# Cross-attention on one core: most of the context turned by VectorE from block loads, Wv turned into a tile of its own, one G product moved ahead of a group of transposes

## The chip, the core and the metric

The kernel runs on one core of a Trainium2 chip. The metric is the device time of one execution in microseconds (us), the median of several runs. One of the executions was also recorded by the hardware profiler; the span of its trace (first to last instruction) is somewhat shorter than the execution's time.

## What is computed

The layer is a cross-attention with eight heads, a residual and a layer norm, all in fp32. There are B = 16 batches, S = 256 queries of DI = 256 features, S2 = 77 context rows of DL = 192 features per batch, and a head size D = 256.

```python
Q = (x @ Wq).reshape(B, -1, H, D).transpose(0, 2, 1, 3)
K = (ctx @ Wk).reshape(B, -1, H, D).transpose(0, 2, 1, 3)
V = (ctx @ Wv).reshape(B, -1, H, D).transpose(0, 2, 1, 3)
score = where(mask, einsum('bhqd,bhkd->bhqk', Q, K) / sqrt(D), -inf)
attn = softmax(score)
out = einsum('bhqk,bhkd->bqhd', attn, V).reshape(B, -1, H * D) @ Wo + x
return layer_norm(out) * gamma + beta
```

The mask is all ones in the inputs, but the kernel reads and applies it.

## The kernel before

The kernel never forms Q, K or V. For each head it forms G = Wk_h Wq_h^T / 16 (192 x 256) and U = Wv_h Wo_h (192 x 256) once. Then a = G^T c^T gives the scores x a, and vw = c U gives what the softmax weights multiply. The 192 context features are split into a part of 128 rows (tiles `gA`, `uA`, `cA`) and a part of 64 rows. In the part of 64 rows two heads share the 128 partitions (`gB`, `uB`), and `cB` holds the 64 context rows twice, in its upper and its lower partitions. So both G and U need their weights turned, and the products need the context turned: features on partitions, (batch, context row) along the free dimension, 16 x 77 = 1232 columns.

Each engine runs its instructions in the order in which the program writes them (a manual schedule), and all loads are issued by SyncE (SP) in program order. At most eight of its transfers are outstanding, since the transfer eight places later waits for the semaphore of the one before. The program has a set-up part and a loop.

The set-up, up to the call of `prepare_last` (L822), goes in this order on TensorE (PE):

- `keep_busy`, then transposes on PE of Wk and Wq of heads 0, 1, 4 and 5: `turn_k`, `turn_q`, `turn_k_last` (one bank of four 128 x 128 transposes each, into PSUM, copied out by `evacuate` at L148, which alternates between ScalarE and VectorE). The G product of heads 0 and 1 (`g_of(0)`) stands after `turn_k(1)`, the transposes of Wk of heads 4 and 5.
- `turn_c(0, first)` (L651): the first three blocks of 112 context rows (`c_sb`, loaded at L568), which hold the first four batches, are turned by six PE transposes, copied to `cA` and the lower half of `cB`, and GpSimd (POOL) copies the lower half to the upper (L668). Then `g_of(1)` and `rest_of_g`.
- the other heads' Wk and Wq were loaded in 32-row blocks (`load_blocks` L563) and are turned by VectorE in 32 x 32 blocks (`turn_blk` L644) into tiles of their own, `kT_blk` and `qT_blk`. `a_of_places((0, 1))` forms a of four heads for batches 0 to 3 (tile `pa`), `of_pair` (L676) and `rest_of_pairs` (L688) form the other G (tiles `pgb`, `phb`), `turn_v` (L670) turns Wv in place, and `a_of_places((2, 3))` follows.
- `turn_c(first, NCR)` (L783): the other eight blocks of context rows are turned by 16 PE transposes (tile `pc`) with eight evacuations and four POOL copies. Then POOL copies the last 13 context rows of every batch to `cRA` and `cRB` (L784, L785), clears `vr` (L786) and makes the mask bias (L790).
- `of_pair` and `rest_of_pairs` again, for U (tiles `pu` and `pw`), with `wvT` as weights. They are copied to `uA` and `uB`; POOL copies each half of `uB` to the other partitions (L809), forms two sums in each of `uA` and `uB` (L812, L813), and finishes the bias (L816 to L818), which also needs a maximum by VectorE (L815).
- VectorE turns the first queries (`transpose_x` L172), and `prepare_last` (L267) multiplies `uA` with `cRA` and `uB` with `cRB` for the last 13 context rows of all batches (tile `pr`: part A of one half of the heads, part B of both, part A of the other) and copies the result to `vr`.

In-place turning of Wv reads and writes every fourth column:

```python
        def turn_v(a):
            blocks = wvT[:, a].rearrange("p m (c n) -> p m n c", n=4)
            nc.vector.transpose(blocks, blocks)
```

and the weights of `pu` and `pw` are then read with a step of four elements (16 bytes):

```python
            return flat(wvT[half(e), a]).rearrange("p (l n) -> p n l", n=4)[:, n]
```

The loop (from L833) takes one batch per turn: `scores` (tile `ps`) of two tiles of 128 queries, the bias and maximum (`shift`), softmax, vw of the batch, a of the next group of four batches, the weighted sum, and the layer norm. The program text of the loop does not differ between the two kernels.

The order of the loads on SP is: Wk and Wq of heads 0, 1, 4, 5 (L571 to L575), the first context blocks (L568), 16 block loads of Wk and Wq (L565), the other context blocks (L568), 16 block loads of Wv (L565), four of Wo (L594), the mask for all 128 partitions (L595), four of the first queries `xT` in 32-row blocks (L168), then `xg` (L144), gamma, beta and the next group's queries.

Of the kernel before, what the change touches and what calls it, by code (L numbers as in the profile page):

```python
# [8 lines left out]
F32 = mybir.dt.float32  # L9
I32 = mybir.dt.int32  # L10
AF = mybir.ActivationFunctionType
ALU = mybir.AluOpType
# [3 lines left out]
P = 128  # L16
H = 8
D = 256
EPS = 1e-05
GB = 4  # L20
KM = 64
MASKED = 3.0e38
# [31 lines left out]
def kernel(  # L54
# [13 lines left out]
    nc = tc.nc  # L68
    B, S, DI = x.shape
    S2, DL = c.shape[1], c.shape[2]  # L70
    LB = DL - P
    CR = 112
    NCR = B * S2 // CR
    NG = B // GB
    QT = S // P
    NT = B * QT
# [5 lines left out]
    NL = DL // BK  # L82
    PW = (NF + 1) * BK
    assert KM == 2 * BK and NM == NF and 2 * KR <= BK
    assert NCR * CR == B * S2 and NG * GB == B and DI == 2 * P and D == 2 * P and 2 * LB == P


    engines = mybir.EngineType
# [33 lines left out]
    vr = const.tile([P, B, DI], F32, tag="vr", name="vr")  # L122
# [144 lines left out]
    def prepare_last():  # L267


        pr = [ps_mm.tile([P, 2, B, KR], F32, tag="mm", name=f"pr_{n}") for n in range(DI // BK)]  # L270

        def part_A(e):
            for n, o in enumerate(pr):
                nc.tensor.matmul(  # L274
                    o[:, e].rearrange("p b k -> p (b k)"),
                    flat(of_e(uA, e)[:, n]),
                    flat(cRA),
                    start=(e == 0),
                    stop=(e == 1),
                )  # L280

        def part_B(e):
            for n, o in enumerate(pr):
                nc.tensor.matmul(  # L284
                    o[:, e].rearrange("p b k -> p (b k)"),
                    flat(of_e(uB, e)[half(n % 2), n]),
                    flat(cRB[half(n % 2)]),
                    start=(e == 1),
                    stop=(e == 0),
                )  # L290
# [253 lines left out]
    early = ctx.enter_context(tc.tile_pool(name="early", bufs=1))  # L544
    pools[0] = turned = early
    with tc.tile_pool(name="wonce", bufs=1) as wp:
        c_sb = wp.tile([CR, NCR, DL], F32, tag="c", name="c_sb")


        wq_nat = wp.tile([P, 2, 2, 2 * D], F32, tag="w128", name="wq_nat")  # L550
# [16 lines left out]
        def load_c(lo, hi):  # L567
            nc.sync.dma_start(c_sb[:, lo:hi, :], c_rows[:, lo:hi, :])  # L568

        first = -(-GB * S2 // CR)  # L570
        nc.sync.dma_start(wk_nat[:, 0], wk_rows[0][:, : 2 * D])  # L571
        nc.sync.dma_start(wq_nat[:, 0], wq_rows[0][:, :, : 2 * D])
        nc.sync.dma_start(wk_nat[:, 1], wk_rows[1][:, : 2 * D])
        nc.sync.dma_start(wq_nat[:, 1], wq_rows[1][:, :, : 2 * D])
        nc.sync.dma_start(wk_last, wk_ends[:, : 2 * D])  # L575
        load_c(0, first)
        for e in range(2):
            load_blocks(wk_blk[:, e], wk_blocks[2 * e + 1])
            load_blocks(wq_blk[:, e], wq_blocks[2 * e + 1])
        load_c(first, NCR)  # L580

        warm = const.tile([P, 1], F32, tag="warm", name="warm")
        nc.scalar.activation(warm, eps, AF.Exp)
# [8 lines left out]
            load_blocks(wvT[:, a], wv_blocks[a])  # L592
        for a in range(NF):
            nc.sync.dma_start(wo_of[a // 2][:, a % 2], wo_rows[a])  # L594
        nc.sync.dma_start(  # L595
            bias_f.bitcast(I32), mask.rearrange("b k -> (b k)").partition_broadcast(P)
        )
# [24 lines left out]
        def turn_q(e, u):  # L622
            chunks = [
                wq_nat[:, e, t, u * D + dc * P : u * D + (dc + 1) * P]
                for dc in range(2) for t in range(2)
            ]
            pt = turn_chunks(chunks, f"q_{e}_{u}")
            evacuate(flat(qT[:, e, u]), flat(pt))

        def turn_k(e):  # L630
            pt = turn_chunks([wk_nat[:, e, n * P : (n + 1) * P] for n in range(4)], f"k_{e}")
            evacuate(
                kT[:, e].rearrange("p u n l -> p (u n) l")[:, :, :P], pt
            )
# [13 lines left out]
                    blk[:, e].rearrange("p m (n c) -> p m n c", c=BK),  # L648
                )

        def turn_c(lo, hi):  # L651
            for r in range(lo, hi, 2):
                n = min(2, hi - r)
                pc = ps_mm.tile([P, 4, P], F32, tag="mm", name=f"pc_{r}")
                for lc in range(2):
                    for j in range(n):
                        nc.tensor.transpose(  # L657
                            pc[:, 2 * lc + j, :CR],
                            c_sb[:, r + j, lc * LB : lc * LB + P],
                            ident[:CR, :CR],  # L660
                        )
                rows = slice(r * CR, (r + n) * CR)
                evacuate(flat(cA)[:, rows].rearrange("p (j m) -> p j m", m=CR), pc[:, :n, :CR])
                evacuate(
                    flat(cB)[LB:, rows].rearrange("p (j m) -> p j m", m=CR),
                    pc[LB:, 2 : 2 + n, :CR],
                )
                nc.gpsimd.tensor_copy(flat(cB)[:LB, rows], flat(cB)[LB:, rows])  # L668

        def turn_v(a):  # L670
            blocks = wvT[:, a].rearrange("p m (c n) -> p m n c", n=4)
            nc.vector.transpose(blocks, blocks)

        def of_pair(out, a, weight, moving):  # L676

            for n in range(4):
                for e in range(2):
                    nc.tensor.matmul(  # L680
                        out[e][:, a % 2, :],
                        weight(a, e, n)[:, :P],
                        moving(a, e, n),
                        start=(n == 0),
                        stop=(n == 3),
                    )
# [23 lines left out]
            return kT_blk[half(e), a, n]  # L710

        def wv_part(a, e, n):
            return flat(wvT[half(e), a]).rearrange("p (l n) -> p n l", n=4)[:, n]

        def wo_part(a, e, n):
            return wo_of[a // 2][half(e), a % 2, n, :]
# [1 line left out]
        def g_of(e):  # L718

            pg = ps_mm.tile([P, 2, DI], F32, tag="mm", name=f"pg_{e}")  # L720
            for u in range(2):
                for dc in range(2):
                    nc.tensor.matmul(
                        pg[:, u],
                        kT[:, e, u, dc, :P],
                        qT[:, e, u, dc],
                        start=(dc == 0),
                        stop=(dc == 1),
                    )
            nc.scalar.mul(gA[:, NF * e : NF * e + 2], pg, D ** -0.5)  # L730
# [23 lines left out]
        keep_busy(4)  # L754
        turn_q(0, 0)
        turn_q(0, 1)
        turn_k(1)
        g_of(0)
        turn_q(1, 0)
        turn_q(1, 1)  # L760
        turn_k_last()
        turn_c(0, first)
        g_of(1)
        rest_of_g(0)
        rest_of_g(1)
# [14 lines left out]
        nc.sync.dma_start(bet, beta.partition_broadcast(P))  # L780
        a_of_places((2, 3))
        turn_v(3)
        turn_c(first, NCR)  # L783
        nc.gpsimd.tensor_copy(cRA, cA[:, :, KM:])  # L784
        nc.gpsimd.tensor_copy(cRB, cB[:, :, KM:])  # L785
        nc.gpsimd.memset(vr, 0.0)  # L786

        nc.gpsimd.tensor_scalar(bias_f, bias_f.bitcast(I32), 0.0, -MASKED, ALU.is_equal, ALU.mult)  # L790

        for j in range(NF // 2):
            pu = two_banks("pu", j)
            for a in range(2 * j, 2 * j + 2):
                of_pair(pu, a, wv_part, wo_part)
            for e in range(2):
                evacuate(
                    of_e(uA, e)[:, :, 2 * j : 2 * j + 2].rearrange("p n a c -> p a n c"),
                    pu[e].rearrange("p a (n c) -> p a n c", c=BK),
                )  # L800
        for j in range(NF // 2):
            for e, pw in enumerate(
                rest_of_pairs(j, (2 * j, 2 * j + 1), wv_part, wo_part, "pw")
            ):
                for i, engine in enumerate((nc.scalar.copy, nc.vector.tensor_copy)):
                    a = 2 * j + i
                    here, there = (of_e(uB, e)[half(k), :, a] for k in (i, 1 - i))
                    engine(here, pw[half(i)].rearrange("p (n c) -> p n c", c=BK))
                    nc.gpsimd.tensor_copy(there, here)  # L809
# [12 lines left out]
        prepare_last()  # L822


# [131 lines left out]
```

## Time and profile before

| what | value |
|---|---|
| median of three runs | 280.88 us (280.25 to 281.27) |
| the profiled execution's own time | 279.81 us |
| span of its trace | 278.0 us |
| granted TensorE clock, mean | 0.993 |
| PE busy | 269.4 us (97%) |
| VectorE (DVE) busy | 206.6 us (74%) |
| ScalarE (ACT) busy | 166.6 us (60%) |
| GpSimd (POOL) busy | 167.8 us (60%) |
| moved by DMA | 22.61 MB |

The profiled execution takes 1.81 us more than its span and 1.07 us less than the median. "L680" is line 680 of the kernel before. PEld is the loading of a matmul's weights, which can run beside the matmul before it; a matmul in fp32 appears as two records. A wait is put down to the semaphore that came last. A DMA's time to landing runs from its issue to its semaphore.

### The profile page before, as it was taken

The numbers are of one execution on the slowest core, as the hardware profiler recorded it, in microseconds if no ns is written. First come the engines' busy times: TensorE is split into PE (matmuls) and PEld (weight loads), VectorE is DVE, ScalarE is ACT, GpSimd is POOL, SyncE is SP. The second block draws the span as 40 slices with busy tenths as digits, with TensorE's granted clock in tenths as the row PEclk, the third lists the DMA queues.
The fourth block names the chain that finished last, engine by engine and source line by source line (L and its number), as shares of the span: only waits on it lengthen the run. The fifth ranks groups of instructions, "written<-read, shape, count | busy, mean of one in ns | idle before, by whom it ended". The sixth has DMA issues, their size and how long they took to land.

```text
span 278.0 us, 13274 instructions
## 1 busy us (share of the span) xinstructions
PE 269.4 (97%) x5924; PEld 194.2 (70%) x5924; DVE 206.6 (74%) x423; ACT 166.6 (60%) x447; POOL 167.8 (60%) x226
## 2 busy tenths in 40 slices
PE   7999999999999999999999999999999999999991
PEld 6756499976595959585868686868677767575650
DVE  0463952777838898878889787778788887788785
ACT  2303232146638676767767676868585857869761
POOL 1000069946677777787877878777777536335274
PEclk9999999999999999999999999999999999999997
DMA  6997999930000100950100109500001010010103
GB/s 192 249 230 154 308 261 238 204 105 4 2 6 2 35 10 24 189 174 4 42 2 5 41 5 193 180 16 22 24 2 42 2 40 14 31 41 2 40 4 113
DMA packets 35641, 22.61 MB, mean 81 GB/s; under 512 B 17712, under 2 KB 34048, under 8 KB 35584
## 3 DMA queue, kind: packets, MB, share of 16 engines
q1 hardware_dynamic: 35440, 21.64, 30.8%
q8 instruction: 46, 0.75, 1.2%
q10 hardware_dynamic: 144, 0.13, 0.1%
q14 instruction: 11, 0.09, 0.1%
HBM read 17.57 MB, written 4.19 MB: 78 GB/s over the span
## 4 chain that ended last, share of the span: by engine, by line
PE 89%; DVE 4%; DMA 3%; ACT 2%; SPq 1%; POOL 0%; issue 0%; POOLq 0%; ACTq 0%
PE ps L313 23%; PE pa L199 12%; PE pv L241 9%; PE po L429 9%; PE pm L429 7%; PE pa L213 6%; PE pv L252 6%; PE po L378 5%; DMA c_sb<-in_ctx_dram 3%; PE pu L680 3%; PE pr L274 2%; ACT e L342 2%; PE pw L694 1%; PE pgb L680 1%; PE pr L284 1%; PE pc L657 1%
## 5 line engine op out<-in xcount | busy, mean ns | idle before, releaser
L342 ACT ACTIVATE e<-s,top 128x77 f32<-128x77 f32 x256 | 67.1, 347 | 52.1 <-DVE top L335 49.9
L356 POOL TENSOR_TENSOR p<-e,rden 128x512 f32<-128x512 f32 x64 | 45.9, 739 | 46.5 <-DVE rden L350 46.3
L313 PE MATMUL ps<-a,xT 128*32 128x154 f32 x2048 | 70.0, 294 | 0.0
L313 PEld LDWEIGHTS ps<-a,xT 128*32 128x32 f32 x2048 | 66.1, 110 | 1.7 <-issue 0.7
L328 DVE TENSOR_TENSOR s<-ps,bias 128x308 f32<-128x308 f32 x64 | 30.3, 475 | 17.6 <-PE ps L313 15.9
L199 PE MATMUL pa<-cA,gA 128*32 128x308 f32 x512 | 35.8, 423 | 0.0
L462 POOL TENSOR_TENSOR xg<-xg,m 128x256 f32<-128x256 f32 x33 | 24.2, 734 | 13.5 <-DVE xg L476 11.8
L199 PEld LDWEIGHTS pa<-cA,gA 128*32 128x32 f32 x512 | 16.4, 110 | 20.9 <-issue 8.0
L241 PE MATMUL pv<-uA,cA 128*32 128x512 f32 x256 | 30.4, 592 | 0.0
L366 DVE STREAM_TRANSPOSE pT<-p 128x640 f32<-128x640 f32 x32 | 25.6, 824 | 2.4 <-POOL p L356 2.4
L348 DVE TENSOR_REDUCE den<-e 128x8 f32<-128x616 f32 x32 | 24.7, 772 | 3.5 <-ACT e L342 3.5
L335 DVE TENSOR_REDUCE top<-s 128x8 f32<-128x616 f32 x32 | 25.4, 795 | 1.1
L668 POOL COPY cB<-cB 64x224 f32<-64x224 f32 (+1 forms) x6 | 1.9, 360 | 35.2 <-DVE cB L153 35.2
L392 POOL TENSOR_TENSOR ts<-vw 128x768 f32<-128x768 f32 x11 | 22.0, 1997 | 0.0
L213 PE MATMUL pa<-cB,gB 64*32 64x308 f32 x512 | 19.5, 420 | 0.0
L378 PE MATMUL po<-vw,pT 128*32 128x256 f32 x320 | 19.2, 380 | 0.0
L863 ACT COPY vw<-pv 128x512 f32<-128x512 f32 x32 | 16.9, 579 | 2.5 <-PE pv L252 2.5
L495 ACT ACT_TABLE_LOAD x14 | 18.0, 1283 | 0.3
L213 PEld LDWEIGHTS pa<-cB,gB 64*32 64x32 f32 x512 | 9.7, 107 | 11.3 <-issue 7.6
L252 PE MATMUL pv<-uB,cB 64*32 64x512 f32 x256 | 17.4, 601 | 0.0
L516 DVE SCALAR_TENSOR_TENSOR xg<-xg,mv,gam 128x256 f32<-128x256 f32 x25 | 17.2, 688 | 0.0
L378 PEld LDWEIGHTS po<-vw,pT 128*32 128x32 f32 x320 | 10.0, 110 | 9.5 <-DVE den L348 2.5
(115 smaller groups left out, 444.0 us busy)
## 6 DMA issues: line engine op xcount, KB each, us to landing
xT<-in_x_dram SPq DMA_DIRECT2D x16, 256.0 KB, 6.1
xg<-in_x_dram SPq DMA_DIRECT2D x4, 1024.0 KB, 7.6
out_dram<-xg SPq DMA_DIRECT2D x15, 256.0 KB, 2.3
wo<-in_L_xattn_Wo_dram SPq DMA_DIRECT2D x4, 512.0 KB, 5.9
wvT<-in_L_xattn_Wv_dram SPq DMA_DIRECT2D x16, 96.0 KB, 3.0
wq_nat<-in_L_xattn_Wq_dram SPq DMA_DIRECT2D x2, 512.0 KB, 6.0
wq_blk<-in_L_xattn_Wq_dram SPq DMA_DIRECT2D x8, 128.0 KB, 4.7
wk_blk<-in_L_xattn_Wk_dram SPq DMA_DIRECT2D x8, 96.0 KB, 5.5
```

The lines of the kernel that those rows point to most:

```text
L199: nc.tensor.matmul(flat(o[i * BK : (i + 1) * BK]), gA[:, h, cols(dc, i)], flat(cA[:, batches, :]), start=not B_first, stop=B_first,)
L213: nc.tensor.matmul(flat(banks[j + k][i * BK : (i + 1) * BK]), gB[half(k), h % NF, cols(dc, i)], flat(cB[half(k), batches, :]), start=B_fir ...
L241: nc.tensor.matmul(pv[k][i * BK : (i + 1) * BK], cA[:, b, k * BK : (k + 1) * BK], uA[:, parts, :, i], start=True, stop=False,)
L252: nc.tensor.matmul(pv[k][i * BK : (i + 1) * BK], cB[half(k), b, k * BK : (k + 1) * BK], uB[half(k), parts, :, i], start=False, stop=True,)
L313: nc.tensor.matmul(ps[m // 2][i * BK : (i + 1) * BK, m % 2 * 2 * S2 : (m % 2 + 1) * 2 * S2], xT_of[g][:, j * NM + m, dc], flat(a_of[g][:, ...
L328: nc.vector.tensor_tensor(s[:, a * H // 2 : (a + 1) * H // 2], ps[a][:, : H // 2 * S2].rearrange("p (h k) -> p h k", k=S2), bias[:, b, :]. ...
L335: nc.vector.tensor_reduce(top, s, AX.X, ALU.max, negate=True)
L342: nc.scalar.activation(e[:, h], s[:, h], AF.Exp, bias=top[:, h : h + 1])
L356: nc.gpsimd.tensor_tensor(part, e_mh[:, :, :, keys], rden_mh.unsqueeze(3).to_broadcast(list(part.shape)), ALU.mult,)
L366: nc.vector.transpose(pT_of[t].rearrange("p n m q -> p m n q"), p.rearrange("p m (n k) -> p m n k", k=BK),)
L378: nc.tensor.matmul(po[i * BK : (i + 1) * BK], pT[:, n, i], vw_of[b][:, 2 - n // 2 * 2 : 4 - n // 2 * 2, n % 2, :] if n < NF else vr[:, b, ...
L429: nc.tensor.matmul(out[i * BK : (i + 1) * BK], weight[:, i], moving, start=(n == 0), stop=(n == len(terms) - 1),)
```

## The change

There are three edits, and some moves that go with them.

1. The context's rest (the 896 rows after the first three blocks of 112) is no longer loaded as rows and turned on PE. Six loads of 32-row blocks, one for each 32 of the 192 features, bring it straight into the columns of `cA` (four loads) and the lower half of `cB` (two loads), in pieces of 32 elements (128 bytes). Two VectorE transposes of 896 columns turn these columns in place, POOL makes the upper half of `cB` by one copy of 64 x 896, and `cRA` and `cRB` follow. The loads stand after those of Wo; the turning stands between the U products of the second pair and their evacuation.
2. `turn_v` writes its result to a new tile `wv_turned`, in which the weights of each product lie side by side. That tile takes the memory of `vr`; `vr` comes into being after U is done, and only the columns that nothing else writes are cleared (6 of every 32), by VectorE instead of POOL.
3. `g_of(0)` stands ahead of `turn_k(1)`.

The bias's first step goes from POOL to VectorE, behind the evacuations of `pu`; POOL's last bias steps go ahead of its sums in `uA` and `uB`.

```diff
@@ loads
+        rest = slice(first * CR, None)
+        def load_rest():
+            blocks = c.rearrange("b k l -> (b k) l")[rest].rearrange("(m r) l -> r m l", r=BK)
+            for l in range(NL):
+                i, of = (l, cA) if l < NM else (l - NM + LB // BK, cB)
+                nc.sync.dma_start(
+                    flat(of)[i * BK : (i + 1) * BK, rest].rearrange("p (m q) -> p m q", q=BK),
+                    blocks[:, :, l * BK : (l + 1) * BK],
+                )
+
+        def turn_rest():
+            nc.vector.transpose(flat(cA)[:, rest], flat(cA)[:, rest])
+            nc.gpsimd.tensor_copy(cRA, cA[:, :, KM:])
+            nc.vector.transpose(flat(cB)[LB:, rest], flat(cB)[LB:, rest])
+            nc.gpsimd.tensor_copy(flat(cB)[:LB, rest], flat(cB)[LB:, rest])
+            nc.gpsimd.tensor_copy(cRB, cB[:, :, KM:])
...
-        load_c(0, first)
+        nc.sync.dma_start(c_sb, c_rows[:, :first, :])
         for e in range(2):
             load_blocks(wk_blk[:, e], wk_blocks[2 * e + 1])
             load_blocks(wq_blk[:, e], wq_blocks[2 * e + 1])
-        load_c(first, NCR)
...
             nc.sync.dma_start(wo_of[a // 2][:, a % 2], wo_rows[a])
+        load_rest()
         nc.sync.dma_start(
             bias_f.bitcast(I32), mask.rearrange("b k -> (b k)").partition_broadcast(P)
         )
@@ Wv
+        wv_turned = const.tile([P, NF, 4, DL], F32, tag="vr", name="wv_turned")
         def turn_v(a):
-            blocks = wvT[:, a].rearrange("p m (c n) -> p m n c", n=4)
-            nc.vector.transpose(blocks, blocks)
+            nc.vector.transpose(
+                wv_turned[:, a].rearrange("p n (m r) -> p m n r", r=BK),
+                wvT[:, a].rearrange("p m (c n) -> p m n c", n=4),
+            )
...
-            return flat(wvT[half(e), a]).rearrange("p (l n) -> p n l", n=4)[:, n]
+            return wv_turned[half(e), a, n]
@@ order
         turn_q(0, 1)
+        g_of(0)
         turn_k(1)
-        g_of(0)
...
         a_of_places((2, 3))
         turn_v(3)
-        turn_c(first, NCR)
-        nc.gpsimd.tensor_copy(cRA, cA[:, :, KM:])
-        nc.gpsimd.tensor_copy(cRB, cB[:, :, KM:])
-        nc.gpsimd.memset(vr, 0.0)
-        nc.gpsimd.tensor_scalar(bias_f, bias_f.bitcast(I32), 0.0, -MASKED, ALU.is_equal, ALU.mult)
         for j in range(NF // 2):
             pu = two_banks("pu", j)
             for a in range(2 * j, 2 * j + 2):
                 of_pair(pu, a, wv_part, wo_part)
+            if j:
+                turn_rest()
             for e in range(2):
                 evacuate(
                     of_e(uA, e)[:, :, 2 * j : 2 * j + 2].rearrange("p n a c -> p a n c"),
                     pu[e].rearrange("p a (n c) -> p a n c", c=BK),
                 )
+        nc.vector.tensor_scalar(bias_f, bias_f.bitcast(I32), 0.0, -MASKED, ALU.is_equal, ALU.mult)
...
-        for u in (uA, uB):
-            t2, _, b22, b11, b12 = (u[:, q].rearrange("p n i c -> p (n i c)") for q in range(5))
-            nc.gpsimd.tensor_tensor(t2, b22, b12, ALU.subtract)
-            nc.gpsimd.tensor_tensor(t2, t2, b11, ALU.add)
         nan = wp.tile([P, B, 1], F32, tag="nan", name="nan")
         nc.vector.tensor_reduce(nan[:, :, 0], bias, AX.X, ALU.max)
         nc.gpsimd.tensor_tensor(nan, nan, nan, ALU.mult)
         nc.gpsimd.tensor_tensor(nan, nan, nan, ALU.subtract)
         nc.gpsimd.tensor_tensor(bias, bias, nan.to_broadcast([P, B, S2]), ALU.add)
+        for u in (uA, uB):
+            t2, _, b22, b11, b12 = (u[:, q].rearrange("p n i c -> p (n i c)") for q in range(5))
+            nc.gpsimd.tensor_tensor(t2, b22, b12, ALU.subtract)
+            nc.gpsimd.tensor_tensor(t2, t2, b11, ALU.add)
         for j in range(0, GT, 2):
             transpose_x(0, j)
+        vr = const.tile([P, B, DI], F32, tag="vr", name="vr")
+        ends = flat(vr).rearrange("p (n c) -> p n c", c=BK)[:, :, 2 * KR :]
+        nc.vector.memset(ends, 0.0)
         prepare_last()
```

More of the change, by code (lines that the diff above doesn't have):

```diff
@@ L72 @@
     CR = 112
-    NCR = B * S2 // CR
     NG = B // GB
@@ L84 @@
     assert KM == 2 * BK and NM == NF and 2 * KR <= BK
-    assert NCR * CR == B * S2 and NG * GB == B and DI == 2 * P and D == 2 * P and 2 * LB == P
+    assert NG * GB == B and DI == 2 * P and D == 2 * P and 2 * LB == P
     engines = mybir.EngineType
@@ L121 @@
     cRB = const.tile([P, B, KR], F32, tag="cRB", name="cRB")
-    vr = const.tile([P, B, DI], F32, tag="vr", name="vr")
     p_ring = [const.tile([P, NM, PW], F32, tag=f"p{i}", name=f"p_{i}") for i in range(2)]
@@ L546 @@
     with tc.tile_pool(name="wonce", bufs=1) as wp:
-        c_sb = wp.tile([CR, NCR, DL], F32, tag="c", name="c_sb")
+        first = -(-GB * S2 // CR)
+        c_sb = wp.tile([CR, first, DL], F32, tag="c", name="c_sb")
         wq_nat = wp.tile([P, 2, 2, 2 * D], F32, tag="w128", name="wq_nat")
@@ L565, in load_blocks @@
                 nc.sync.dma_start(to[i * BK : (i + 1) * BK], blocks[i])
-        def load_c(lo, hi):
-            nc.sync.dma_start(c_sb[:, lo:hi, :], c_rows[:, lo:hi, :])
-        first = -(-GB * S2 // CR)
+        rest = slice(first * CR, None)
+        assert (B * S2 - first * CR) % BK == 0
+        def load_rest():
[12 more added lines that the diff above has]
+            nc.gpsimd.tensor_copy(cRB, cB[:, :, KM:])
         nc.sync.dma_start(wk_nat[:, 0], wk_rows[0][:, : 2 * D])
@@ L649, in turn_blk, with turn_c @@
                 )
-        def turn_c(lo, hi):
-            for r in range(lo, hi, 2):
-                n = min(2, hi - r)
+        def turn_c():
+            for r in range(0, first, 2):
+                n = min(2, first - r)
                 pc = ps_mm.tile([P, 4, P], F32, tag="mm", name=f"pc_{r}")
@@ L761 @@
         turn_k_last()
-        turn_c(0, first)
+        turn_c()
         g_of(1)
```

## The prediction

> **What bounds the kernel now.** I read the chain of work that ended last first, because a busy share says nothing of which wait ends last. PE has 89% of it. These are its pieces in order of time (start, length, what; all us):
>
> ```profile
> 3.12 8.36 DMA c_sb<-in_ctx_dram
> 11.48 0.04 issue
> 11.53 0.80 PE pc L657 x6
> ...
> 22.46 3.65 PE pgb L680 x32
> ...
> 34.52 1.68 PE pc L657 x16
> 36.20 7.77 PE pu L680 x64
> 43.98 3.68 PE pw L694 x64
> 47.65 3.01 PE pr L274 x16
> 50.66 3.01 PE pr L284 x32
> 53.68 3.01 PE pr L274 x16
> 56.69 4.33 PE ps L313 x128
> ```
>
> Up to 11.53 the chain is the load of the first context blocks. From there to 258 each PE piece begins where the one before it ends, so an instruction taken off PE in that stretch shortens the span by its own length, if what follows it is ready that much sooner. The piece at 34.52 is the 16 transposes that go.
>
> Then the groups by line, shapes kept apart, of the stretch 0 to 62 us (busy us, mean ns of one, idle before):
>
> ```profile
> L680 PE MATMUL pu<-wo,wvT 64*128 64x256 f32 x64 | 7.8, 400 | 0.0
> L680 PEld LDWEIGHTS pu<-wo,wvT 64*128 64x128 f32 x64 | 7.5, 325 | 0.1
> L672 DVE STREAM_TRANSPOSE wvT<-wvT 128x768 f32<-128x768 f32 x4 | 6.4, 1644 | 0.0
> L680 PE MATMUL pgb<-qT_blk,kT_blk 64*128 64x256 f32 x32 | 3.7, 382 | 0.0
> L680 PEld LDWEIGHTS pgb<-qT_blk,kT_blk 64*128 64x128 f32 x32 | 3.0, 187 | 0.8 <-ACT a L151 0.5
> L646 DVE STREAM_TRANSPOSE kT_blk<-wk_blk 128x768 f32<-128x768 f32 x2 | 1.9, 950 | 0.0
> ```
>
> `pu` and `pgb` are the same products but for the weights' step of four elements in `pu`: its weight loads take 325 ns and not 187, and in the chain one of its matmuls takes 7.77/64 = 121 ns and not 3.65/32 = 114. The transposes of L672 and L646 differ in the same way.
>
> Last, the timeline and the busy time by stage (length, PE, PEld, DVE, ACT, POOL, clock, DMA share, GB/s) for what must supply PE:
>
> ```profile
> 42.77 4.39 POOL L790 TENSOR_SCALAR bias<-bias 128x1232 f32<-128x1232 int32 x1
> 47.21 3.59 POOL L809 COPY uB<-uB 64x256 f32<-64x256 f32 x8
> ```
>
> ```profile
> 24.00:26.00 2.00, 2.00 (x20) 1.55 (x16) 0.00 (x0) 0.00 (x0) 0.00 (x0) 1.00 0.26 69
> 26.00:28.00 2.00, 2.00 (x38) 1.20 (x40) 0.00 (x0) 1.09 (x2) 0.00 (x0) 1.00 0.59 161
> 34.00:36.00 2.00, 2.00 (x33) 1.54 (x16) 1.96 (x4) 1.67 (x5) 0.00 (x0) 1.00 1.03 413
> 38.00:40.00 2.00, 2.00 (x20) 2.00 (x20) 0.03 (x1) 0.00 (x0) 1.94 (x5) 1.00 1.37 173
> ```
>
> POOL's eight `uB` copies begin only after its 4.39 us of bias and end at 50.8, just as part B of `pr` (50.66) needs them: a PE that is earlier finds them late unless POOL is relieved too. The DMA engines are nearly idle from 24 to 28, and a stretch of 256-byte pieces (38 to 40, `xT`) moves 173 GB/s where big pieces move 413.
>
> [...]loads 74% longer cost only 6% of spacing. [...]The trace has 512-byte pieces at 228 GB/s (mean of 14 to 22 us), which is 16 x 512/228 = 36 ns per piece and engine, and 256-byte pieces at 177 GB/s (38 to 44), 23 ns; none of 128 bytes.
>
> **The change, part by part.**
>
> *The 16 transposes go.* 1.68 us of PE on the path. Their eight evacuations and four POOL copies lay beside it. What is next: `pu` at 34.52 needs Wo, turned Wv and two free banks. Wo arrives at about 30.4 (below). The three Wv transposes that precede the `a` copies on DVE begin at 28.73 and end by 33.7 at today's price; the first `a` copies, 0.42 to 0.46 us, free both banks by 34.2. Nothing is late: -1.68.
>
> *Wv in a tile of its own.* `pu` at the spacing of `pgb`: 64 x 114 = 7.30 us, -0.47. `pw` today has 3.68/64 = 57 ns, and its like with contiguous weights (`phb`, 1.89/32 = 59) is no faster: 0. Bounds: 0 (if the spacing has another reason) and -0.6. I take -0.47. The DVE transposes still read with the step, write without it: 950 to 1644 ns, beside PE either way.
>
> *G of heads 0 and 1 earlier.* Today PE works from 7.26 to 11.02 and then waits 0.51 for the context blocks. Moved ahead, `pg` waits for the copy of `qT`, which ends at 7.44 on DVE and 7.78 on ACT. If all of it waits for the second, the same 3.76 us end at 11.54, as the load lands: 0, worst +0.1. Without the load as cover it could save 0.3.
>
> *The loads.* On SP the one context load ahead of Wv goes, six come behind Wo, ahead of mask, `xT`, `xg`, gamma and beta. The old one is 0.69 MB, 3.0 us at 228 GB/s; without it the eight-transfer limit no longer holds Wv back (SP waits 3.0 us for it today), so the idle 2.3 us (0.74 and 0.41 of two 2 us windows) fill too. Wo ends today at about 35.7 (413 GB/s holds until then), hence at 30.4. The new loads are 6 x 896 = 5376 pieces. Price per piece and engine: on the line through 36 and 23 ns it is 16; [...]no cheaper than 256 bytes, 23[...]. I take 23: 5376 x 23/16 = 7.7 us. `cA` (two thirds) is in at 35.5, `cB` at 38.1, the mask (1.6 us) at 39.7, `xT` (5.9 us) at 45.6. xg, gamma, beta and the second `xT` are used after 75 us: covered.
>
> *DVE, at the new times* (`pu` 34.5 to 41.8, `pw` to 45.5, `pr` B at 48.5, `ps` at 54.5). `uA` copy until 38.9; the turn of 896 columns costs 950 + 128 x 1.07 (slope to the 1225 ns of 1024 columns) = 1.09 us, twice: 40.0 and 41.1; `uA` 41.9 to 42.6; bias on DVE [...]1.44 us (the reduce of the same 1232 columns), I take 1.4: 44.0; four `uB` copies (0.42) are done 1.2 us after `pw` ends, 46.7; maximum 1.44, four `xT` turns 0.67 each: 50.9; clearing 768 columns 0.66 at POOL's 3.51 us for 4096, I take 0.8: 51.7. `vr` copies, first 0.6 us, must precede `ps`: slack 2.2. So cA is needed at 38.9, cB at 40.0, the mask at 42.6, xT at 48.2: slack 3.4, 1.9, 2.9 and 2.6. Queued behind a late load would be `uA`, bias and `uB` copies, for which `pr` waits.
>
> *POOL.* `vr` clearing (3.51) and bias (4.39) go. `cRA` 0.36 at 40.4; the `cB` copy of 896 columns 1.09 (283 ns for 112, 398 for 224) at 42.2; `cRB` 42.6; eight `uB` copies of 0.40 from 44.2: 47.4, needed 48.5, slack 1.1. Then two small steps and the bias (2.25) by 51.0, needed 56.7; the `uA` sums by 53.6, needed 58.9; the `uB` sums by 56.1, needed 62.7. All covered: 0.
>
> *Sum.* -1.68 - 0.47 = -2.15. The profiled execution of 279.81 (span 278.0) would be 277.66 (span 275.85). It lies 1.07 below the median; from the median, 280.88 - 2.15 = 278.7.
>
> **The rivals.** (a) Only the transposes pay; `pu` keeps 121 ns: 279.2. For it: weight loads overlap and matmuls of 393 ns hide much. Against: `pgb` with the same matmul has 114. (b) The cover is partly gone: pieces at 37 to 43 ns, or DVE later by 1 to 3 us than reckoned, eat a part: 278.7 to 280.9, middle 279.9. (c) Slower: the small pieces cost the doubled 46 ns. The six loads take 15.5 us, `cB` is in at 45.9, and on POOL its turn, copy, `cRB` and eight copies (1.09 + 1.09 + 0.36 + 3.2) follow: `pr` B begins at 51.6, not 48.5. `xT` comes at 53.4, its turns, clearing and first copy end at 57.5: the same delay. 3.1 lost against 2.15 gained: 281.8. Loss begins at 37 ns and outweighs the gain from 43 ns. [...]Against: 256-byte pieces[...] cost less than 512-byte ones. (d) A little more than the sum, by spacing or a start on an earlier load: 278.1.
>
> **How the numbers follow.** Forecast 0.67 (278.2 to 279.3, with the spread of runs), (a) 0.12, (b) 0.10, (c) 0.07, (d) 0.04. From 277.9 to 279.9 lie forecast, (a), (d) and half of (b), 0.88; closer ends would cut into the bounds of `pu` and the run spread. A measurement can tell 0.3% (0.84 us) from no change: faster than 280.04 are forecast, (a), (d) and half of (b), 0.88; half of (b) and a part of (c) within, 0.07; slower 0.05.
>
> **What would show it.** `pu` should begin near 34.5 straight after `pa` and take 7.3; weight loads near 187 ns; DVE should wait for no load ahead of its turns; `pr` B follow A with no gap; `ps` begin near 54.5. Wrong: a DVE wait on `cA`, `cB`, `bias` or `xT`, a gap ahead of `pr` or `ps`, or `pc` later than 11.6.

## The result, and the profile after

The changed kernel takes 278.28 us (median of six runs, 277.25 to 279.10), the kernel before in the same session 280.69 (280.25 to 281.27). The ratio is 0.9907 with a 95% interval of 0.9884 to 0.9931: 2.41 us less. The forecast from 280.88 was 278.7, range 277.9 to 279.9. The profiled execution took 277.25 us with a span of 275.5 (before: 279.81 and 278.0; reckoned: 277.66 and 275.85), at a mean granted clock of 0.995. Executions over 1.5% above the fastest of their kernel count as a slower state and are left out of the figures below: three of 22 with the bias on POOL, three of 20 with the spare loads, and one of the kernel before, at 992 us.

The chain of the work that ended last, after the change (start, length, what; us):

```profile
3.13 8.38 DMA c_sb<-in_ctx_dram
...
11.56 0.79 PE pc L673 x6
...
22.49 3.65 PE pgb L701 x32
...
34.55 7.11 PE pu L701 x64
41.66 3.61 PE pw L715 x64
45.28 3.01 PE pr L272 x16
48.29 3.01 PE pr L282 x32
51.30 3.01 PE pr L272 x16
54.31 4.32 PE ps L311 x128
```

The start and the stretch up to 34.5 are as before. The piece of 16 transposes is gone and nothing has taken its place: `pu` follows `pa` directly. `pu` has become 0.66 shorter and `pw` 0.07. The scores begin at 54.31 instead of 56.69, 2.38 earlier: -1.68 - 0.66 - 0.07, and +0.03 from the start. From there to its end this trace takes 221.2 us (275.5 - 54.31), the one before 221.3.

The groups of 0 to 62 us, shapes kept apart (busy us, mean ns of one, idle before):

```profile
L701 PE MATMUL pu<-wo,wv_turned 64*128 64x256 f32 x64 | 7.2, 379 | 0.0
L690 DVE STREAM_TRANSPOSE wv_turned<-wvT 128x768 f32<-128x768 f32 x4 | 6.2, 1600 | 0.0
L701 PEld LDWEIGHTS pu<-wo,wv_turned 64*128 64x128 f32 x64 | 6.1, 187 | 1.2 <-ACT a L149 0.5
```

A weight load of `pu` takes 187 ns instead of 325, the price of `pgb`. But the four VectorE turns of Wv still take 1600 ns each (1644 before), although they now write contiguously.

Last, the timeline of the new supply (start, length, what, idle before), and SP's issue of the loads:

```profile
38.89 1.10 DVE L581 STREAM_TRANSPOSE cA<-cA 128x896 f32<-128x896 f32 x1
40.02 1.11 DVE L583 STREAM_TRANSPOSE cB<-cB 64x896 f32<-64x896 f32 x1
42.46 0.80 DVE L818 TENSOR_SCALAR bias<-bias 128x1232 f32<-128x1232 int32 x1
44.09 3.58 POOL L827 COPY uB<-uB 64x256 f32<-64x256 f32 x8 [1.49 <-ACT uB L826]
48.22 3.08 PE L282 MATMUL pr<-cRB,uB 64*128 64x208 f32 x32
49.01 2.49 DVE L173 STREAM_TRANSPOSE xT<-xT 128x512 f32<-128x512 f32 x4 [1.05 <-DMA xT<-in_x_dram]
```

```profile
15.91 9.51 SPq L564 DMA_DIRECT2D wvT<-in_L_xattn_Wv_dram  x16
25.46 1.86 SPq L609 DMA_DIRECT2D wo<-in_L_xattn_Wo_dram  x4
27.37 7.23 SPq L575 DMA_DIRECT2D cA<-in_ctx_dram  x4
34.64 1.83 SPq L575 DMA_DIRECT2D cB<-in_ctx_dram  x2
36.52 0.54 SPq L611 DMA_DIRECT2D bias<-in_mask_BxS_if_dram  x1
```

DVE waits for none of `cA`, `cB` and the mask, but for `xT`, 1.05 us. Such a wait was one of the prediction's signs of being wrong; here it costs PE nothing. POOL ends the `uB` copies at 47.67, 0.55 before part B of `pr` needs them.

### The profile page after: what moved, and what is told of

Read it like the earlier page. It is cut to its first block, busy times and chain, and to the rows that moved or that the text cites. A ratio compares the mean times of both kernels' runs of the same rounds, so it can differ in the third digit from the quotient of the medians.

```text
span 275.5 us, 13238 instructions
## 1 busy us (share of the span) xinstructions
PE 267.7 (97%) x5908; PEld 192.2 (70%) x5908; DVE 208.9 (76%) x423; ACT 165.4 (60%) x443; POOL 159.5 (58%) x221
## 4 chain that ended last, share of the span: by engine, by line
PE 89%; DVE 4%; DMA 3%; ACT 2%; SPq 1%; POOL 1%; issue 0%; POOLq 0%; ACTq 0%
PE ps L311 24%; PE pa L197 12%; PE pv L239 9%; PE po L427 9%; PE pm L427 8%; PE pa L211 6%; PE pv L250 6%; PE po L376 5%; DMA c_sb<-in_ctx_dram 3%; PE pu L701 3%; PE pr L272 2%; ACT e L340 2%; PE pgb L701 1%; PE pw L715 1%; PE pr L282 1%; PE phb L715 1%
## 5 line engine op out<-in xcount | busy, mean ns | idle before, releaser
L326 DVE TENSOR_TENSOR s<-ps,bias 128x308 f32<-128x308 f32 x64 | 30.4, 475 | 17.6 <-PE ps L311 17.5
L197 PEld LDWEIGHTS pa<-cA,gA 128*32 128x32 f32 x512 | 17.2, 110 | 20.1 <-issue 7.7
L884 ACT COPY a<-pa 128x308 f32<-128x308 f32 x48 | 16.6, 447 | 0.0
```

What stands on the lines that cost most here:

```text
L197: nc.tensor.matmul(flat(o[i * BK : (i + 1) * BK]), gA[:, h, cols(dc, i)], flat(cA[:, batches, :]), start=not B_first, stop=B_first,)
L326: nc.vector.tensor_tensor(s[:, a * H // 2 : (a + 1) * H // 2], ps[a][:, : H // 2 * S2].rearrange("p (h k) -> p h k", k=S2), bias[:, b, :]. ...
L884: nc.scalar.copy(dst, src)
```

## The experiments

The theory: the gain is the 16 transposes (1.68) and the closer spacing of `pu`, on a path where PE never waits; it holds only while the small loads, DVE's queue and POOL's copies stay under cover. The rivals: the transposes alone pay; or the loads or POOL are the real limit. Medians of one kernel differ by some tenths of a us from the runs' spread, and the start differs more: `pc` begins at anything from 11.24 to 13.68 us, as the first loads land. So where a trace can tell, I compare the stretch from the first `pc` to the first `ps`; it is 54.31 - 11.56 = 42.75 us in the changed kernel and 56.69 - 11.53 = 45.16 us in the kernel before, 2.41 less. The medians, too, differ by 2.41 us (280.69 and 278.28). For a median of an experiment the kernel before of the same session is given beside it.

**Wv turned in place again** (weights with a step of four elements; all else as changed).

```diff
-            nc.vector.transpose(
-                wv_turned[:, a].rearrange("p n (m r) -> p m n r", r=BK),
-                wvT[:, a].rearrange("p m (c n) -> p m n c", n=4),
-            )
+            blocks = wvT[:, a].rearrange("p m (c n) -> p m n c", n=4)
+            nc.vector.transpose(blocks, blocks)
...
-            return wv_turned[half(e), a, n]
+            return flat(wvT[half(e), a]).rearrange("p (l n) -> p n l", n=4)[:, n]
```

> The kernel after the change, with Wv turned in place and read with the step of four again; the rest of the change stays. My theory: the step costs TensorE 10 ns on each of the 64 matmuls of pu, and nothing else waits for it; pu takes 7.7 to 7.8 us where the kernel after has 7.11, pw about 3.68 where it has 3.61, and the time is 0.6 to 0.8 us above that of the kernel after, about 279.0 us. Rival: the shorter pu of the kernel after comes from its start (no transposes ahead of it, other banks) and not from the step; then pu stays at 7.1 and the time at 278.3 us.

Measured: 278.63 us (278.33 to 279.29; before 280.37), ratio to before 0.9932 (0.9912 to 0.9951). Its chain:

```profile
12.27 0.79 PE pc L673 x6
...
35.26 7.77 PE pu L698 x64
43.03 3.68 PE pw L712 x64
...
55.74 4.33 PE ps L311 x128
```

From `pc` to `ps` 43.47 us, 0.72 more than the changed kernel, all of it in `pu` and `pw`. The groups show weight loads of 325 and 192 ns again instead of 187 and 133. So the own tile is worth 0.72 us on the path, and the rival that only the transposes pay falls in the trace. The medians point the same way, a gain of 1.74 us over the kernel before instead of 2.41, but the intervals of the two ratios overlap, and they could not have told it.

**The rest of the context on PE again** (row loads, `turn_c(first, NCR)` ahead of `pu`; Wv's tile, the order of G and POOL's relief stay).

```diff
-        load_rest()
...
+        load_c(first, NCR)
...
         turn_v(3)
+        turn_c(first, NCR)
+        nc.gpsimd.tensor_copy(cRA, cA[:, :, KM:])
+        nc.gpsimd.tensor_copy(cRB, cB[:, :, KM:])
...
-            if j:
-                turn_rest()
```

> The kernel after the change, with the context's rest loaded as rows and turned by 16 transposes of TensorE again; Wv in its own tile, the order of G, the bias's first step on VectorE and POOL's relief stay. My theory: the 16 transposes lie on the path with all of their 1.68 us, so the time is 1.6 to 1.8 us above that of the kernel after, about 280.0 us, and scores begin at 56.0 us in the trace. Rival: part of the gain came from POOL's relief and the other order of its work, which this kernel keeps; then it gives back less, 0.8 to 1.2 us, about 279.3 us.

Measured: 279.44 us (278.77 to 279.71; before 280.37), ratio 0.996 (0.9944 to 0.9976). Its chain:

```profile
11.24 0.79 PE pc L657 x6
...
34.24 1.68 PE pc L657 x16
...
55.68 4.32 PE ps L311 x128
```

From `pc` to `ps` 44.44, which is 1.69 more: the transposes' own length and nothing else. What this kernel keeps over the kernel before is 45.16 - 44.44 = 0.72, which is Wv's tile alone: the bias step on DVE and the smaller clearing, which stayed, gave nothing by themselves. Together the two edits make 2.41. The median would have left the rival standing, since it lies 1.16 us above 278.28, within the 0.8 to 1.2 that the rival gave. Against the kernel before of its own session the gain is 0.93 instead of 2.41, a loss of 1.48.

**G of heads 0 and 1 behind the transposes again.**

```diff
-        g_of(0)
         turn_k(1)
+        g_of(0)
```

> The kernel after the change, with G of heads 0 and 1 behind the transposes of Wk of heads 4 and 5 again. My theory: the start ends with the landing of the first context blocks, so the transposes of the context begin at 11.5 us either way and the time stays within 0.2 us of the kernel after, 278.3 us. Rival: where the second Wk load is late, the order matters; then this kernel is 0.3 us or more slower, 278.6 us or above.

Measured: 278.67 us (277.19 to 280.58; before 280.37), ratio 0.9927 (0.99 to 0.9955). The median is what the rival asked for, but the executions spread over 3.4 us, and the trace speaks for the theory. The edit acts ahead of `pc`, and there PE stands waiting for the context load in either order, 0.50 us here and 0.21 in the changed kernel; from `pc` to `ps` it is 42.75 us, as there. The trace also holds a wait of DVE:

```profile
11.77 0.79 PE L673 MATMUL pc<-ident,c_sb 112*128 112x112 f32 x6 [0.50 <-DMA c_sb<-in_ctx_dram]
...
44.00 0.80 DVE L818 TENSOR_SCALAR bias<-bias 128x1232 f32<-128x1232 int32 x1 [1.36 <-DMA bias<-in_mask_BxS_if_dram]
```

The mask was 1.36 us late for DVE, and `xT` 1.43, and PE lost nothing: so much cover is left behind them.

**The bias's first step back on POOL.**

```diff
-        nc.vector.tensor_scalar(bias_f, bias_f.bitcast(I32), 0.0, -MASKED, ALU.is_equal, ALU.mult)
+        nc.gpsimd.tensor_scalar(bias_f, bias_f.bitcast(I32), 0.0, -MASKED, ALU.is_equal, ALU.mult)
```

> The kernel after the change, with the bias's first step issued to POOL at the same place of the program. My theory: POOL takes 4.4 us for it as in the kernel before, behind the copy of cRB at 42.6, so the eight copies of uB begin at 47.0 and end at 50.6 us, where part B of pr wants them from 48.2: part B begins at 49.7 or later and the time is 1.5 to 2.4 us above that of the kernel after, 279.8 to 280.7 us. Rival: part B can follow the copies closely, or VectorE, relieved of 0.8 us, gives something back; then the loss is under 0.8 us, about 278.9 us.

Measured: 280.35 us (278.64 to 282.29; before 280.37), ratio 1.0006 (0.9988 to 1.0024): the whole gain is gone. The timeline shows how:

```profile
43.94 4.38 POOL L818 TENSOR_SCALAR bias<-bias 128x1232 f32<-128x1232 int32 x1
48.39 3.59 POOL L827 COPY uB<-uB 64x256 f32<-64x256 f32 x8
51.12 3.08 PE L282 MATMUL pr<-cRB,uB 64*128 64x208 f32 x32 [1.84 <-POOL uB L827]
```

The `uB` copies stand behind the bias on POOL, and PE waits 1.84 us for them; from `pc` (12.55) to `ps` (57.21) it is 44.66, 1.91 more than changed. So the move of this step, which looks like tidying, is a condition of the gain, although it gains nothing by itself.

**Four more loads of 128-byte pieces** into a spare tile, ahead of the rest's own (the same result, more DMA work).

```diff
+        spare = wp.tile([P, B * S2 - first * CR], F32, tag="spare", name="spare")
+        blocks = c.rearrange("b k l -> (b k) l")[rest].rearrange("(m r) l -> r m l", r=BK)
+        for l in range(NM):
+            nc.sync.dma_start(
+                spare[l * BK : (l + 1) * BK].rearrange("p (m q) -> p m q", q=BK),
+                blocks[:, :, l * BK : (l + 1) * BK],
+            )
         load_rest()
```

> The kernel after the change with four loads more, of the same 128-byte pieces, into a spare tile that nothing reads, issued just ahead of the loads of the context's rest; the rest is unchanged. It measures what is left of the cover. My theory: in the kernel after, the pieces cost 17 ns each, but SP issues them slowly, the loads arrive just when VectorE wants them, and only 1.3 us are left before the first vr copies (behind the turns of xT) delay the scores. Four loads cost 3.9 us (engines) to 7.2 us (issue), so scores begin 2.5 to 5.8 us later and the time is 281 to 284 us. Rival: the slack is as the prediction had it, 2.6 us ahead of the turns of xT and 2.2 behind; then the loss is 0 to 2.4 us, 278.3 to 280.7 us.

Measured: 280.99 us (278.47 to 282.61; before 280.26), ratio 1.002 (1.0 to 1.004), at the lower edge of what was expected. The end of its chain, and DVE's wait from its timeline:

```profile
41.91 6.41 DMA bias<-in_mask_BxS_if_dram
48.34 0.91 DVE bias L825
49.27 0.44 DVE uB L833
...
52.03 3.08 PE pr L282 x32
...
58.13 3.91 PE ps L311 x113
```

```profile
28.68 9.39 SPq L613 DMA_DIRECT2D spare<-in_ctx_dram  x4
44.86 1.11 DVE L581 STREAM_TRANSPOSE cA<-cA 128x896 f32<-128x896 f32 x1 [5.32 <-DMA cA<-in_ctx_dram]
```

SP needs 9.39 us more, DVE stands 5.32 us for `cA` and 0.50 for the mask, which holds up the `uB` copies queued behind it on DVE. From `pc` (12.13) to `ps` it is 46.00, 3.25 more than changed and within the 2.5 to 5.8 expected. That is the loss of rival (c), 3.1, made real by the kind of route the prediction gave. It took ten such loads to get there and not six, so a piece costs less than the 46 ns of that rival. What gave way was not the `vr` copies, as expected, but the `uB` copies.

**A faster start, in five tries.** If the loads and the start were improved, was more to be had? The first (label `e6_wo_by_act`) issues Wo from ScalarE's queue in the middle of the set-up, to let SP reach the context's rest sooner, and clears `vr` ahead of the `xT` turns.

```diff
-        for a in range(NF):
-            nc.sync.dma_start(wo_of[a // 2][:, a % 2], wo_rows[a])
-        load_rest()
...
         a_of_places((0, 1))
+        for a in range(NF):
+            nc.scalar.dma_start(wo_of[a // 2][:, a % 2], wo_rows[a])
+        load_rest()
...
```

> The kernel after the change, with the four loads of Wo issued by ScalarE behind its copies of a, so that SP goes from Wv to the context's rest at once, and with vr cleared ahead of the turns of xT. My theory: the loads behind Wv come about 2 us earlier, the waits of VectorE for xT and mask vanish, and as none of them lies on the path the time stays within 0.3 us of the kernel after, 278.3 us. Rival: a part of the path still waits for loads in most executions; then this is 0.5 us or more faster, 277.8 us or less. Another: ScalarE is held up by the issue and its copies come late; then it is slower.

Measured: 282.96 us (281.96 to 283.59; before 280.26), ratio 1.0092 (1.0068 to 1.0116). A miss, slower than the kernel before, and neither rival's reason is the one that the timeline shows:

```profile
16.47 18.47 SPq L564 DMA_DIRECT2D wvT<-in_L_xattn_Wv_dram  x16
23.02 2.37 ACTq L784 DMA_DIRECT2D wo<-in_L_xattn_Wo_dram  x4
...
34.43 2.98 DVE L683 STREAM_TRANSPOSE wv_turned<-wvT 128x768 f32<-128x768 f32 x2 [3.59 <-DMA wvT<-in_L_xattn_Wv_dram]
...
37.83 8.86 PE L694 MATMUL pu<-wo,wv_turned 64*128 64x256 f32 x62 [2.22 <-DVE a L151]
```

Wo's large transfers went out while Wv's small ones were still being issued. Wv's issue took 18.47 us instead of 9.51, DVE stood 3.59 us for it, and PE 2.22 us for the `a` copies behind DVE's turns, after the first two matmuls of `pu`.

That is not all. Right behind this wait of PE the clock that TensorE was granted falls, as the windows show (length, PE, PEld, DVE, ACT, POOL, clock, DMA share, GB/s):

```profile
38.00:40.00 2.00, 2.00 (x16) 1.73 (x18) 2.00 (x4) 0.00 (x0) 0.00 (x0) 0.79 1.38 153
40.00:42.00 2.00, 2.00 (x12) 1.60 (x12) 0.38 (x1) 0.00 (x0) 0.00 (x0) 0.50 1.16 229
42.00:44.00 2.00, 2.00 (x20) 1.77 (x18) 0.73 (x2) 0.59 (x1) 0.00 (x0) 0.86 1.02 249
```

The 62 matmuls took 8.86 us, where the same 62 take 7.17 in the third try below, whose trace has a mean granted clock of 0.998. So of the 4.59 us that this trace has more from `pc` (11.99) to `ps` (59.33), some 1.7 are the lower clock (8.86 - 7.17) and 2.22 the wait for Wv's turns. The changed kernel's trace has 1.00 throughout the set-up.

The second (`e9_first_by_dve`) turns the first context columns on DVE as well, from block loads, so that the six `pc` transposes go, too:

```diff
+        ahead = slice(0, -(-first * CR // BK) * BK)
...
-        nc.sync.dma_start(c_sb, c_rows[:, :first, :])
+        load_rest(ahead, range(NM))
...
+                load_rest(ahead, range(NM, NL))
...
         def turn_c():
-            for r in range(0, first, 2):
-...
+            nc.vector.transpose(flat(cA)[:, ahead], flat(cA)[:, ahead])
+            nc.vector.transpose(flat(cB)[LB:, ahead], flat(cB)[LB:, ahead])
+            nc.gpsimd.tensor_copy(flat(cB)[:LB, ahead], flat(cB)[LB:, ahead])
```

> The kernel after the change, with the first context blocks too loaded in 32-row blocks (352 rows) and turned by VectorE, so that no PE transposes of the context are left. My theory: TensorE saves 0.8 us and no longer waits for the landing of the first context rows (0.2 us), but six loads in place of one push all later loads back by 1 to 2 us, and the cover of 1.3 us ahead of the scores is used up: the time is between 277.5 and 279.0 us. Rival: the context's turns in VectorE's queue wait for loads and hold up the turns of Wk and Wq behind them, and the other G product comes late; then it is slower than the kernel after by over 1 us.

Measured: 302.52 us (301.52 to 302.96). A fault of mine: blocks of 32 rows end at column 352 and the rest begins at 336, and the rest's load stood ahead of the turn in program order. The turn therefore waited 25.61 us for the rest's load, and context rows 320 to 367 come out mixed, in this kernel alone. It says nothing on the theory.

The third (`e8_first_by_dve_wo_by_act`) joins both edits, with the rest's loads behind the first turn.

> The two edits before together: the first context blocks turned by VectorE too, Wo issued by ScalarE, vr cleared ahead of the turns of xT. My theory: the cover that the second edit gives back holds the later loads, so the 0.8 us of transposes and the wait at the start are kept: 0.8 to 1.2 us below the kernel after, 277.1 to 277.5 us. Rival: the start is bound by the loads of Wk and Wq and not by TensorE, and the small pieces among them delay it; then no gain, 278.3 us or more.

Measured: 282.71 us (280.25 to 284.23; before 280.26), ratio 1.0079 (1.0057 to 1.0101), again a miss. The start did gain (`pa` at 14.54 instead of 15.90 in the timelines), but Wo on ScalarE's queue again stretched Wv's issue, to 15.85 us, and `pu` waited 2.37 behind the turn of Wv. Its `ps` begins at 56.39, 2.08 late. This trace is of the fastest execution, at 280.25 us; the three fastest, up to 280.92, had a mean granted clock of 0.998 or 0.999, the other fourteen, from 281.92 on, 0.989 to 0.993. My estimate, from the median and this execution (282.71 - 280.25 = 2.46), is that most executions lost some 2 us more to a lower clock, as in the first try, but none of these has a trace. Why PE was slowed behind a wait of 2.22 us there (62 matmuls in 8.86 us) and not behind one of 2.37 here (7.17) stays open.

The fourth (`e10_first_by_dve_rest_behind`) leaves Wo on SP: the edit of the second, with the rest, mask and `xT` issued behind the first turn, and `vr` cleared ahead of the `xT` turns.

```diff
         turn_c()
+        load_rest()
+        nc.sync.dma_start(
+            bias_f.bitcast(I32), mask.rearrange("b k -> (b k)").partition_broadcast(P)
+        )
+        load_xT(0)
```

> The kernel after the change with the first context blocks turned by VectorE too (352 rows, six loads), with the loads of the context's rest written behind these turns, so that the turns do not depend on them, and with vr cleared ahead of the turns of xT. Wo stays on SP. My theory: TensorE loses the last 0.8 us of context transposes and the wait for the first rows, 1.0 to 1.4 us as the start of the run with Wo by ScalarE showed, and the loads behind Wv come no later than in the kernel after, as the run with the false dependency showed: scores begin at 53.0 to 53.3 us and the time is 277.0 to 277.4 us. Rival: with PE 1 us earlier the mask and xT, which come just in time, are now late and take most of it back: 278.0 us or more.

Measured: 278.77 us (277.34 to 279.54; before 280.46), ratio 0.9931 (0.9907 to 0.9956): no better than the changed kernel, as the rival had it. From its timeline:

```profile
14.97 4.61 PE L197 MATMUL pa<-cA,gA 128*32 128x308 f32 x64
...
33.81 7.18 PE L684 MATMUL pu<-wo,wv_turned 64*128 64x256 f32 x64
...
40.62 1.11 DVE L582 STREAM_TRANSPOSE cA<-cA 128x896 f32<-128x896 f32 x1 [2.32 <-DMA cA<-in_ctx_dram]
...
48.14 3.08 PE L282 MATMUL pr<-cRB,uB 64*128 64x208 f32 x32 [0.53 <-POOL uB L815]
...
54.17 4.39 PE L311 MATMUL ps<-a,xT 128*32 128x154 f32 x128
```

The start gained 0.93 on the profiled execution of the changed kernel, `pu` still 0.67 (33.81 against 34.48 there). But the small loads at the front pushed the others back: `cA` came 2.32 us late for DVE, `cB` a further 0.36 and the mask 0.43, and PE waited 0.53 for the `uB` copies behind them. `ps` is ahead by 0.07 (54.24 there) and begins about 1 us later than expected.

The fifth (`e11_bias_behind`) puts the bias step behind the `uB` copies on DVE, so that the mask holds up nothing.

```diff
-        nc.vector.tensor_scalar(bias_f, bias_f.bitcast(I32), 0.0, -MASKED, ALU.is_equal, ALU.mult)
         for j in range(NF // 2):
             for e, pw in enumerate(
...
+        nc.vector.tensor_scalar(bias_f, bias_f.bitcast(I32), 0.0, -MASKED, ALU.is_equal, ALU.mult)
         nan = wp.tile([P, B, 1], F32, tag="nan", name="nan")
```

> The kernel of the run before with the bias's first step behind the copies of uB on VectorE, so that a late mask holds up nothing that TensorE waits for. My theory: where the mask is late this saves up to 0.5 us, else nothing: 276.8 to 277.3 us, with less spread than the run before. Rival: the step then delays the turns of xT and the vr copies, and scores begin later: 0.3 us or more above the run before.

Measured: 278.5 us (276.96 to 279.93; before 280.46), ratio 0.9926 (0.9899 to 0.9954), above the range expected. In its trace the wait ahead of part B of `pr` is 0.27 and `ps` begins at 53.59, 0.65 ahead. From there to its end the trace then takes 224.0 us against 221.2. PE stands 0.87 us in the first `pv` at 59.26 and 0.82 in `po` at 121.2, waits that the trace of the changed kernel lacks. The DVE turns of `xT` in this trace end at 54.6, later than the 51.5 there; whether the first of these waits comes from that I did not test, and the second and the other 1.1 us stay unexplained.

**The changed kernel once more**, beside these two.

> The kernel after the change, unchanged, beside the two others on the same chip, so that they can be compared with it directly: 278.3 us, with scores beginning between 54 and 55 us in the trace, as the first context rows land between 11.2 and 12.3 us from run to run.

Measured: 278.24 us (276.5 to 279.51), ratio 0.9918 (0.9888 to 0.9948); before 280.46. The median is as expected; the scores begin at 56.43, not between 54 and 55. The profiled execution had a span of 277.7, 2.2 more than the first, and its chain shows where that lies:

```profile
3.14 10.50 DMA c_sb<-in_ctx_dram
...
13.68 0.79 PE pc L673 x6
...
56.43 4.33 PE ps L311 x128
```

The first context load landed 2.12 us later; from `pc` to `ps` it is 42.75 again. So the gain is the same in an execution with a late start. Between these two executions of one kernel the landing of the first loads is nearly the whole difference; of the others there is no trace. No version that I ran beats the changed kernel by more than the spread.

## Why the prediction was right, point by point

- *The 16 transposes, -1.68*: right, 1.68 in the chain and 1.69 by putting them back.
- *Wv's own tile, -0.47*: that the weights' step costs spacing was right (weight loads of 325 and 187 ns), the size too small. Putting it back costs 0.72. I took `pgb`'s spacing of 114 ns, length over count, for `pu`, twice as long a stretch. The two stretches of the same product, 3.65 us for 32 and 7.11 us for 64, give 3.46/32 = 108 ns for one more matmul and 0.19 us that each stretch has once; `phb` and `pw`, 1.89 us for 32 and 3.61 for 64, give 54 ns and 0.17 in the same way. `pu` before, 7.77, is then 118 ns apiece. A mean over a short stretch holds what comes once, and I carried that over twice; what it consists of no run shows. `pw`, taken at nothing by the same mean, gave 0.07.
- *G earlier, 0*: right; PE waits for the context load in either order.
- *The loads*: the result, that they cost nothing, was right, the path to it was not, and part of it was luck. Of two errors one made up for a part of the other. The piece was too dear: from 34 to 36 us, at a mean DMA share of 1.06, the context's rest moved 118 GB/s, from which I estimate 16 x 128/118 = 17 ns per piece and engine, against the 23 taken. The line through the two sizes of the trace before gave 16 (its 36 ns came from a stretch that also holds the context's rows, of 768 bytes): better than my caution, and the doubled price, 46, does not show. Yet the loads came later than reckoned, since I put the arrival of Wo at 30.4; its last load was issued at 26.9 and took 7.7 to land, 34.6, just after `pu` had begun. That cost nothing only because `pu` takes Wo load by load, and the first had landed at 29.3 (25.5 + 3.8). I had read the end of Wo before (35.7) from the throughput; by its own issue and landing it was 30.3 + 7.5 = 37.8. And Wv's issue still took 9.51 us, with the DMA engines busy by 0.45 to 0.77 from 18 to 26 us, so that the idle stretch did not fill as reckoned. In all, `cA` and the mask came 2.5 and 2.6 us later than reckoned, `cB` 1.4 to 1.9 and `xT` about 3.4.
- *DVE's queue*: its order and times were right within 0.1 us at `cA` and `cB` (38.89 and 40.02 against 38.9 and 40.0). The slack was not. The last load of `cA` was in by 38.0 (issued at 33.2, 4.8 to land), `cB`'s by 39.5 to 40.0, the mask at 42.3, against needs of 38.9, 40.0 and 42.5: slack of 0.9, at most 0.5, and 0.1, where 3.4, 1.9 and 2.9 were reckoned, and `xT` was 0.8 after its reckoned need of 48.2. That nothing was late ahead of the `uB` copies in this execution was luck, and that it did not matter in others is cover that the prediction had not counted: DVE could wait a while at no cost. Its waits ahead of the `uB` copies (`cA`, `cB`, mask) were 0 here, 1.36 with G behind, 3.11 with the first columns on DVE (the fourth try) and 5.82 with the spare loads; PE lost 0, 0, 0.53 and 3.25. The last two differences, 3.11 - 0.53 and 5.82 - 3.25, both give 2.6 us of lateness that is free there, and none of the waits for `xT` up to 1.43 was paid. The bias took 0.80 on DVE, not the 1.4 taken from the reduce of the same 1232 columns (1.44).
- *POOL*: right, with half the slack. The `uB` copies ended at 47.67 (47.4 reckoned, slack 0.55 and not 1.1), and without the relief the gain is gone.
- *The sum, -2.15*: -2.41 from `pc` to `ps`, of which `pu` and `pw` make the 0.26 more. Of the rivals (a) falls by the Wv run, (c) by 17 ns, and (b) did not occur in this kernel, though the spare loads show it a few us away.

The windows on which the piece's price rests (length, PE, PEld, DVE, ACT, POOL, clock, DMA share, GB/s):

```profile
24.00:26.00 2.00, 2.00 (x20) 1.57 (x18) 0.00 (x0) 0.00 (x0) 0.00 (x0) 1.00 0.45 125
...
34.00:36.00 2.00, 2.00 (x36) 1.38 (x16) 1.96 (x4) 0.86 (x3) 0.00 (x0) 1.00 1.06 118
...
38.00:40.00 2.00, 2.00 (x22) 1.78 (x22) 1.71 (x2) 0.59 (x1) 0.00 (x0) 1.00 0.50 177
```

The first and the last show half-idle DMA engines while loads are still to come; the middle one has a share of 1.06, at 118 GB/s where the stretch 30 to 32 has 389.

## What to carry to other kernels

Work taken off the bounding engine is worth its own length only if every other supplier of the next product is that much sooner (here 2.41 us, of which 1.91 were lost with the bias on POOL), so go through the queues of the helpers (here POOL's copies behind its bias) and relieve them in the same change. Price a matmul stream by the difference between two lengths, not by the mean of the short one. For a load, take the landing of the last transfer ahead of it from its issue and its time to landing, and not only the price of its pieces. Where a change makes TensorE wait, look at the granted clock behind the wait before putting the whole loss down to the wait (in the first try 2.22 us were the wait and some 1.7 the clock).

## What the runs showed of the hardware that was not expected

- A DVE turn of 768 fp32 columns that reads with a step of four elements takes 1600 ns even when it writes contiguously (1644 with both strided, 950 with neither): nearly all of the price came with the read. The write side paid 44 ns on top of a read with the step, and a write with the step alone was not run.
- Four loads of Wo, 512 KB each, on ScalarE's queue stretched the issue of Wv's 16 loads on SP from 9.51 to 18.47 us.
- Behind a wait of TensorE of 2.22 us in the first try its granted clock read 0.79, 0.50 and 0.86 in three windows of 2 us, and 62 matmuls took 8.86 us; behind one of 2.37 us in the third try's trace, of mean granted clock 0.998, the same 62 took 7.17.
- The step from int32 to fp32 on 128 x 1232 took 0.80 us on DVE and 4.38 on POOL.
